# Graph attention on one core: the order of the last two node tiles in layer 2

## The chip, the cores and the metric

The kernel runs on one core of one Trainium2 chip. Its time is the device time of one execution in microseconds (us). Several executions are timed; the median of them is the figure for a kernel, and one further execution is taken with the hardware profiler. Times inside the trace are counted from the first instruction of the program.

## The reference

Two graph-attention (GAT) layers over 3125 nodes and 53125 edges (25000 random pairs in both directions and a self loop for each node, sorted by destination), with a normalisation ahead, a residual product in each layer, and the input added at the end. Cut to what matters:

```python
edge_index = jnp.stack([src, dst])
h = jnp.maximum(_layernorm(x), 0.0)
x = x + _L0_gnn_ref(h, edge_index, ...)

def _L0_gnn_ref(x, ei, ...):
    h0 = x
    h = relu(layer_norm(gat_conv(x, ei, W1, a_src1, a_dst1, b1, heads=4, out_ch=256, concat=True), g1, be1))
    h1 = h + (h0 @ Wr1 + br1)                                   # 3125 x 1024
    h = layer_norm(gat_conv(h1, ei, W2, a_src2, a_dst2, b2, heads=1, out_ch=768, concat=False), g2, be2)
    return h + (h1 @ Wr2 + br2)                                 # 3125 x 768

def gat_conv(x, ei, W, a_src, a_dst, bias, heads, out_ch, concat):
    xl = (x @ W).reshape(n, heads, out_ch)
    # ei as above plus one more self loop for each node
    e = leaky_relu(alpha_src[src] + alpha_dst[dst], 0.2)
    e = exp(e - segment_max(e, dst)[dst])
    alpha = e / (segment_sum(e, dst)[dst] + 1e-16)
    return segment_sum(xl[src] * alpha[:, :, None], dst) + bias
```

## The kernel before, in words

Everything is float32 where it matters here. The nodes are cut into 25 tiles: tiles 0 to 23 have 128 rows, tile 24 has the 53 that are left (`NB`=25, `LAST`=53). Each tile's incoming edges lie in slots of 128 edges: 17 slots for a full tile, 8 for tile 24. Tiles come in chains of three (0,1,2), ..., (21,22,23), (24): within a chain the last slot of a tile is also slot 0 of the next, so it is gathered once.

Layer 1 and the preparation of both layers are untouched by the change. Layer 2 is one block of code at the end, in which the orders of the tensor engine (PE), the vector engine (DVE) and the scalar engine (ACT) are those of the program text (`manual_schedule`). The transfers issued by SP and the indirect gathers issued by POOL are written in the same text and wait by semaphores. The parts of layer 2:

- `residuals`: a generator, one step for each of 8 slices of the product h1 @ Wr2 of a tile. `filled(n)` takes n steps; the loop takes 0, 1, 1, 2 and 4 of them after the five rounds of a tile (`STEPS`), always three tiles ahead (`AHEAD`). Full tiles use `dense` as whole matmuls (L190), tile 24 as 32- and 21-column pieces (L194). It also issues the loads of later h1 and x rows.
- `fetch`: gathers rows of `table2` (768 features and the source score) into a ring of 36 buffers, in the order of the list `slots_due`, on POOL (L210, L214).
- `values`: ACT copies each slot's source score into `slots[b % 2]` (L1365).
- `softmax`: PE transposes the scores (L1383), DVE adds the mask `pen` and takes the maximum (L1387 to L1390, L1392), ACT takes the exponentials (L1391, L1394, L1395). `penalty` prepares the next tile's mask. After a pause PE transposes the weights (L1399); after another DVE and ACT copy them to `w` (L1402, L1403).
- `summed(b, k)`: round k of five: PE sums the gathered rows by their weights into `pa` (L1426). A full tile has 80 of these matmul records in the trace, tile 24 has 36.
- `totals2`: three short DVE operations on the sums of the weights (L1460 to L1462).
- `finish`: a generator: DVE adds the node's own share (L1439) and, after a pause, the bias (L1441), statistics (L514, L516), ACT takes a square root (L520), DVE applies the norm and adds the residual (L1444, L1445), and the result is stored from ACT's queue (L231). For tile 24 the own share was already scaled and given its bias, so that one operation for each half does it (L1449), then L1454 and L1455.
- `own_share`: two POOL operations that scale tile 24's own rows and add the bias (L1467, L1468).
- `load_own`: SP loads a tile's own rows into the one `own` buffer; tile 24's go into a buffer of h1.

The loop over tiles is 0, 1, ..., 24. While tile b is summed, the softmax of b+1 is made at round 2 and its weights are copied after round 4, and `finish(b-1)` runs in pieces at rounds 0, 1 and 2. The step before the last tile is different: in the text of tile 23, tile 24's softmax is begun ahead of round 0 and its weights are copied after round 1. Exponential and square root use different tables of ACT; a table load (`ACT_TABLE_LOAD`) stands where the function changes.

Of the kernel before, what the change touches and what calls it, by code (L numbers as in the profile page):

```python
# [69 lines left out]
def in_order(  # L70
# [1167 lines left out]
    with tc.tile_pool(name="m2", bufs=1, reuse_waits="tile") as mp, \  # L1238
            tc.tile_pool(name="pg2", bufs=1, space=PSUM, reuse_waits="tile") as pp:
        AHEAD = 3  # L1240
        STEPS = [0, 1, 1, 2, 4]
        RING = 36
        f = C2 // 2

        def small(shape, name, dt=F32, bufs=1):
            return mp.tile(shape, dt, name=name, bufs=bufs)
# [59 lines left out]

        def residuals():

            for b in range(NB):
                h1, xr = h1s.pop(b), xrs[b]  # L1310
                r = rows_of(b)
                pm = pp.tile([P, 2, 512], F32, name="pr")
                for k in range(NK2):
                    if k < NK2 // 2:
                        load_h1(b + 2, ks=slice(2 * k, 2 * k + 2))
                    if k in (3, 4):
                        load_xr(b + 1, slice((k - 3) * f, (k - 2) * f))
                    for i in range(2):
                        dense(pm[:, i, :f], h1[:, k, :], wr2[:, k, i * f:(i + 1) * f], r,
                              start=(k == 0), stop=(k == NK2 - 1), at=half_at(b, i).start)  # L1320
                    if k == NK2 - 1 and r == P:
                        nc.vector.tensor_add(pm[:, :, :f], pm[:, :, :f], halves(ball_b))  # L1322
                        nc.vector.tensor_add(halves(xr), pm[:, :, :f], halves(xr))  # L1323
                    elif k == NK2 - 1:
                        nc.vector.tensor_add(xr[:r], xr[:r], ball_b[:r])
                        for i in range(2):
                            cs = slice(i * f, (i + 1) * f)
                            nc.vector.tensor_add(xr[:r, cs], pm[half_at(b, i), i, :f], xr[:r, cs])
                    yield
# [3 lines left out]
        def filled(n):  # L1333
            for _ in range(n):
                next(fill, None)

        gs = {}
        slots_due = [(b, j) for b in range(NB) for k in ROUNDS for j in k
                     if j < tiles_of(b) and not (j == 0 and shared(b))]
        order_of = {s: i for i, s in enumerate(slots_due)}  # L1340
        asked, unused = 0, set(range(len(slots_due)))
# [20 lines left out]
        def values(b, k):  # L1362
            for j in ROUNDS[k]:
                if (b, j) in gs:
                    nc.scalar.activation(slots[b % 2][:, POS[j], :], gs[b, j][:, C2:C2 + 1].to_broadcast([128, 32]), AF.Copy)  # L1365

        def penalty(b):
            if b < NB:
                pen = pens[b] = pens.get(b) or small([128, WIN], "pen")
                nc.scalar.activation(pen, hots.pop(b), AF.Identity, bias=below, scale=BIG)  # L1370
                nc.scalar.activation(pen, pen, AF.Identity, bias=asad2[:, b, 1:2])
                load_hot(b + 2)

        shares = {}

        def softmax(b):

            nonlocal e0, w0
            at, pen = slots[b % 2], pens.pop(b)
            mix = pp.tile([128, 1024], F32, name="mix")  # L1380
            for c in range(WIN // 128):
                o = FROM[c % 4] + c // 4
                nc.tensor.transpose(mix[:, c * 128:(c + 1) * 128], at[:, o:o + 4].rearrange("p q n -> p (q n)"), ident)  # L1383
            top = small([P, 1], "top", bufs=2)
            e, e0 = e0 or small([P, WIN], "e"), None
            sums_ = mix[:, :WIN]
            nc.vector.tensor_tensor_reduce(out=sums_, in0=sums_, in1=pen, scale=1.0, scalar=-BIG,  # L1387
                                           op0=OP.add, op1=OP.max, accum_out=top)
            nc.vector.tensor_scalar(top, top, both[:, b:b + 1], -1.0, op0=OP.max, op1=OP.mult)
            nc.vector.scalar_tensor_tensor(top, top, SLOPE, top, op0=OP.mult, op1=OP.min)  # L1390
            nc.scalar.activation(e, sums_, AF.Copy, scale=SLOPE)  # L1391
            nc.vector.tensor_tensor(e, sums_, e, OP.max)  # L1392
            v = small([P, 4], "v", bufs=3)
            nc.scalar.activation(e, e, AF.Exp, bias=top, accum_out=v[:, 0:1])  # L1394
            nc.scalar.activation(v[:, 1:2], self_s[:, b:b + 1], AF.Exp, bias=top)  # L1395
            penalty(b + 1)
            yield
            for c in range(WIN // 128):
                nc.tensor.transpose(mix[:, c * 128:(c + 1) * 128], e[:, c * 128:(c + 1) * 128], ident)  # L1399
            yield  # L1400
            w, w0 = w0 or small([128, WIN], "w", bufs=2), None
            nc.vector.tensor_copy(w[:, :512], mix[:, :512])  # L1402
            nc.scalar.activation(w[:, 512:], mix[:, 512:WIN], AF.Copy)  # L1403
            shares[b] = w, v
# [26 lines left out]
        def finish(b, pa):  # L1431

            nonlocal z0
            r = rows_of(b)
            own, v = owns.pop(b), shares.pop(b)[1][:r]
            z, z0 = (z0 or small([P, C2], "z", bufs=2))[:r], None
            if b < NB - 1:
                p = pa[:, :, :f]
                nc.vector.scalar_tensor_tensor(p, halves(own), v[:, 2:3], p, op0=OP.mult, op1=OP.add)  # L1439
                yield  # L1440
                nc.vector.scalar_tensor_tensor(p, p, v[:, 3:4], halves(b2_b), op0=OP.mult, op1=OP.add)  # L1441
                yield from norm_steps(mp, p, C2, 1)
                mu, rstd = norm_steps.found
                nc.vector.scalar_tensor_tensor(p, p, mu, halves(g2_b), op0=OP.subtract, op1=OP.mult)  # L1444
                nc.vector.scalar_tensor_tensor(halves(z), p, rstd, halves(xrs.pop(b)), op0=OP.mult, op1=OP.add)  # L1445
            else:
                for i in range(2):
                    cs = slice(i * f, (i + 1) * f)
                    nc.vector.scalar_tensor_tensor(z[:, cs], pa[half_at(b, i), i, :f], v[:, 3:4], own[:r, cs],  # L1449
                                                   op0=OP.mult, op1=OP.add)  # L1450
                yield
                yield from norm_steps(mp, z, C2, 1)
                mu, rstd = norm_steps.found
                nc.vector.scalar_tensor_tensor(z, z, mu, g2_b[:r], op0=OP.subtract, op1=OP.mult)  # L1454
                nc.vector.scalar_tensor_tensor(z, z, rstd, xrs.pop(b)[:r], op0=OP.mult, op1=OP.add)  # L1455
            store_rows(nc.scalar, out, b, z)
# [4 lines left out]
            nc.vector.tensor_scalar(v[:, 3:4], v[:, 0:1], v[:, 2:3], 1e-16, op0=OP.add, op1=OP.add)  # L1461
            nc.vector.reciprocal(v[:, 3:4], v[:, 3:4])  # L1462

        def own_share(b):
            r = rows_of(b)
            own, v = owns[b][:r], shares[b][1][:r]
            nc.gpsimd.tensor_scalar(own, own, v[:, 2:3], v[:, 3:4], op0=OP.mult, op1=OP.mult)  # L1467
            nc.gpsimd.tensor_tensor(own, own, b2_b[:r], OP.add)  # L1468

        with tc.manual_schedule(engines={PE, ACT, DVE}):  # L1470
            penalty(0)
# [12 lines left out]
            values(1, 0)  # L1484
            values(1, 1)
            ending = iter(())
            for b in range(NB):
                pa = pp.tile([P, 2, 512], F32, name="pa", bufs=2)
                opened = set()
                last = b + 1 == NB - 1  # L1490
                for k in range(len(ROUNDS)):
                    if last and k == 0:
                        load_own(b + 1)
                        for i in range(2, len(ROUNDS)):
                            values(b + 1, i)
                        made = softmax(b + 1)
                        next(made)
                    summed(b, k, pa, opened)
                    if k < 2:
                        next(ending, None)  # L1500
                        if 0 < b < NB - 1:
                            load_own(b, slice(k * f, (k + 1) * f))
                    if b + 1 < NB and not last:
                        if k < 3:
                            values(b + 1, k + 2)
                        if k == 2:
                            made = softmax(b + 1)
                            next(made)
                    if k == 2:
                        for _ in ending:  # L1510
                            pass
                    if k == 4:
                        ending = finish(b, pa)
                        next(ending)
                    if b + 1 < NB and k == (1 if last else 4):
                        next(made)
                        next(made, None)
                        totals2(b + 1)
                        if last:
                            own_share(b + 1)  # L1520
                    filled(STEPS[k])
                if b + 2 < NB:
                    values(b + 2, 0)
                    values(b + 2, 1)
            for _ in ending:
                pass

# [471 lines left out]
```

## Time and profile before

| what | value |
|---|---|
| median of 3 timed runs | 1967.19 us |
| the three runs | 1967.47, 1967.19, 1962.85 us |
| the profiled execution | 1958.36 us, span 1956.5 us |
| mean granted PE clock in it | 0.939 |
| busy: PE, DVE, ACT, POOL | 89%, 51%, 23%, 44% of the span |
| DMA | 539.49 MB, mean 276 GB/s |

The span is the time from the first to the last instruction. Layer 2 stands at the end of it, and the two tiles that the change exchanges are worked on in its last 45 us. A row of a timeline has the start and the duration in us, the engine, the line of the kernel, the operation, what it writes and reads, the shape, and how many instructions were merged; in brackets is the idle time of the engine before it and what ended it. PEld are weight loads, and an engine's name with a q is its queue (a transfer that it issues).

### The profile page before, as it was taken

To read this page: it belongs to the slowest core of one execution; us is meant where nothing else is said; L and a number is where in the kernel's file an instruction comes from. 1 tells how busy PE (TensorE), PEld (TensorE's weight loads), DVE (VectorE), ACT (ScalarE), POOL (GpSimd) and SP (SyncE) were. 2 spreads that over 40 slices of the span, in tenths; PEclk is the share of its full clock that TensorE was granted. 3 is DMA by queue.
4 is the path that set the end of the run, shared out by engine and by line. 5 is a ranking of instruction groups with operands and counts; after the bars stand their busy time and mean duration, and the time that the engine had idled before them with its cause. 6 is when DMAs were issued, how large, how long until landed. Compare 5 with 4: busy or idle time off the path is not lost. (4 is left out here: it accounts for less than half of the span.)

```text
span 1956.5 us, 31270 instructions
## 1 busy us (share of the span) xinstructions
PE 1748.2 (89%) x11522; PEld 967.2 (49%) x11522; DVE 1006.5 (51%) x2604; ACT 451.1 (23%) x1312; POOL 854.9 (44%) x892
## 2 busy tenths in 40 slices
PE   8999998999889899899999998938888888888885
PEld 5666665665555454555655544423333334333332
DVE  7673436888654463555655564402334343433436
ACT  2222430001212121211221211212332332333232
POOL 2000112000465544656666666154555565556662
PEclk9999998999899988899999998969888999889897
DMA  7823557331899897999999998596999999899984
GB/s 237 289 96 119 135 162 258 124 120 50 302 369 341 294 349 258 346 345 397 379 381 361 367 382 313 179 345 212 304 301 299 317 321 318 295 315 311 319 284 136
DMA packets 186339, 539.49 MB, mean 276 GB/s; under 512 B 31571, under 2 KB 80083, under 8 KB 186050
## 3 DMA queue, kind: packets, MB, share of 16 engines
q0 software_dynamic: 97328, 379.74, 54.9%
q1 hardware_dynamic: 84456, 147.27, 21.9%
q10 hardware_dynamic: 4394, 10.39, 1.4%
q8 instruction: 94, 1.54, 0.3%
q14 instruction: 67, 0.55, 0.1%
HBM read 483.81 MB, written 65.62 MB: 281 GB/s over the span
## 5 line engine op out<-in xcount | busy, mean ns | idle before, releaser
L210 POOL DMA_INDIRECT g<-table,idx_s x393 | 377.6, 961 | 494.5 <-DVE al L624 175.7
L214 POOL DMA_INDIRECT g<-table,hi_s x407 | 417.8, 1027 | 288.2 <-PE pa L781 134.1
L190 PE MATMUL pr<-wr,h 128*128 128x384 f32 x768 | 288.0, 520 | 28.7 <-DVE xr L1323 22.3
L1426 PE MATMUL pa<-g,w 128*32 128x384 f32 x1956 | 232.6, 524 | 73.4 <-issue 68.1
L781 PE MATMUL pa<-g,w 128*32 128x256 f32 x3912 | 270.5, 392 | 30.5 <-issue 25.2
L190 PE MATMUL p<-w,h1T 128*128 128x384 f32 (+1 forms) x768 | 268.8, 497 | 0.9 <-issue 0.8
L190 PEld LDWEIGHTS pr<-wr,h 128*128 128x128 f32 x768 | 149.6, 205 | 147.0 <-issue 76.8
L781 PEld LDWEIGHTS pa<-g,w 128*32 128x32 f32 x3912 | 124.1, 111 | 168.3 <-issue 81.5
L190 PEld LDWEIGHTS p<-w,h1T 128*128 128x128 f32 x768 | 140.4, 190 | 115.3 <-issue 25.3
L1426 PEld LDWEIGHTS pa<-g,w 128*32 128x32 f32 x1956 | 65.2, 113 | 216.5 <-issue 207.5
L758 DVE TENSOR_TENSOR w<-oh,al 128x128 f32<-128x128 f32 (+1 forms) x416 | 131.7, 317 | 63.9 <-PE pa L781 26.1
L190 PE MATMUL pr<-h0k,wr 128*128 128x256 f32 (+1 forms) x576 | 150.7, 407 | 4.7 <-issue 3.6
L1033 PE MATMUL pm<-h0g,wr 128*128 128x512 f32 x288 | 133.2, 610 | 0.3 <-issue 0.3
L190 PE MATMUL pm<-w,h0g 128*128 128x344 f32 x432 | 131.7, 460 | 0.3 <-ACT h0g L867 0.3
L190 PEld LDWEIGHTS pr<-h0k,wr 128*128 128x128 f32 x576 | 110.5, 199 | 38.4 <-issue 16.5
L190 PE MATMUL pm<-w,h0l 128*128 128x344 f32 x432 | 129.5, 454 | 0.0
L757 DVE TENSOR_SCALAR oh<-iota_f,rel_s 128x32 f32<-128x32 f32 (+1 forms) x416 | 114.5, 275 | 2.9 <-issue 2.6
L1229 DVE COPY asad<-p 128x2 f32<-128x2 f32 (+1 forms) x25 | 4.0, 160 | 201.4 <-ACT row L1227 175.0
L964 POOL DMA_DIRECT2D hot_d<-ohd x25 | 13.4, 536 | 213.0 <-DVE own L531 128.6
L190 PEld LDWEIGHTS pm<-w,h0g 128*128 128x128 f32 x432 | 81.6, 193 | 40.2 <-issue 1.7
L1322 DVE TENSOR_TENSOR pr<-pr,ball_b 128x768 f32<-128x768 f32 x24 | 23.2, 965 | 149.2 <-PE pr L190 72.6
L190 PEld LDWEIGHTS pm<-w,h0l 128*128 128x128 f32 x432 | 80.5, 190 | 39.1 <-issue 0.2
(295 smaller groups left out, 1769.0 us busy)
## 6 DMA issues: line engine op xcount, KB each, us to landing
s<-slo_d SPq DMA_DIRECT2D x25, 544.0 KB
table<-row SPq DMA_DIRECT2D x24, 512.0 KB
own<-table SPq DMA_DIRECT2D x24, 512.0 KB
h1T_d<-h1T SPq DMA_DIRECT2D x24, 512.0 KB
h<-h1T_d SPq DMA_DIRECT2D x88, 128.0 KB
table<-row SPq DMA_DIRECT2D x24, 392.0 KB
ring<-in_x_dram SPq DMA_DIRECT2D x24, 384.0 KB
out_dram<-z ACTq DMA_DIRECT2D x24, 384.0 KB
```

The costliest lines, as they stand in the source:

```text
L190: nc.tensor.matmul(out_, lhsT, rhs, start=start, stop=stop)
L210: nc.gpsimd.indirect_dma_start(out=g, out_offset=None, in_=table[:, :], in_offset=bass.IndirectOffsetOnAxis(ap=idx_s[:, c], axis=0))
L214: nc.gpsimd.indirect_dma_start(out=g, out_offset=None, in_=table[:, :], in_offset=bass.IndirectOffsetOnAxis(ap=idx_k[:, c], axis=0), bound ...
L757: nc.vector.tensor_scalar(oh, iota_f[:, lo:hi], rel_s[:, c:c + 1], None, op0=OP.is_equal)
L758: nc.vector.tensor_tensor(w, oh[:, None, :].to_broadcast([128, heads, hi - lo]), al[:, POS[j], :, b:b + 1].to_broadcast([128, heads, hi - ...
L781: nc.tensor.matmul(pa[p0:p0 + 32, o // f, o % f:o % f + n], w[:, o // cols, :], g[:, o:o + n], start=to not in opened, stop=False, skip_gr ...
L964: nc.gpsimd.dma_start(hot_d[b], ohs[b])
L1033: nc.tensor.matmul(pm, wr1[:, k, m * 128:(m + 1) * 128], groups[gi][:, k, :], start=(k == 0), stop=(k == NK1 - 1))
L1229: nc.vector.tensor_copy(asad2[:r, b, :], pm[half_at(b, i), 384:n])
L1322: nc.vector.tensor_add(pm[:, :, :f], pm[:, :, :f], halves(ball_b))
L1426: nc.tensor.matmul(pa[p0:p0 + 32, i, :f], w_, g[:, i * f:(i + 1) * f], start=(i, q) not in opened, stop=False, skip_group_check=True)
```

## The change

Layer 2 goes through the tiles in a list `ORDER` = 0, ..., 22, 24, 23; `turn(b, n)` is the tile n places after b, and all that was b+1 or b+2 (gathers, residuals, h1 and x loads, masks, scores) follows the list. The special handling of the step ahead of tile 24 is gone: its softmax stands where every tile's does, and its own share is now made by DVE after its totals. For tile 23, which is now the last, all scores, the softmax, the totals and the own share (on POOL) stand in the text behind tile 24's sums and behind the whole of `finish(24)`. A square root whose result nothing reads, `early`, stands in that softmax behind the exponentials. In `finish(23)` a single operation adds the own share, and the result is made and stored in two column halves, the first from ACT's queue, the second from SP's.

```diff
+        ORDER = [*range(NB - 2), NB - 1, NB - 2]
+        at_turn = {b: i for i, b in enumerate(ORDER)}
+        def turn(b, n):
+            i = at_turn[b] + n
+            return ORDER[i] if i < NB else NB
...
-            for b in range(NB):
+            for b in ORDER:
-                        load_h1(b + 2, ks=slice(2 * k, 2 * k + 2))
+                        load_h1(turn(b, 2), ks=slice(2 * k, 2 * k + 2))
-                        load_xr(b + 1, slice((k - 3) * f, (k - 2) * f))
+                        load_xr(turn(b, 1), slice((k - 3) * f, (k - 2) * f))
...
-        slots_due = [(b, j) for b in range(NB) for k in ROUNDS for j in k
+        slots_due = [(b, j) for b in ORDER for k in ROUNDS for j in k
...
             if b < NB - 1:
                 p = pa[:, :, :f]
-                nc.vector.scalar_tensor_tensor(p, halves(own), v[:, 2:3], p, op0=OP.mult, op1=OP.add)
-                yield
-                nc.vector.scalar_tensor_tensor(p, p, v[:, 3:4], halves(b2_b), op0=OP.mult, op1=OP.add)
+                if b == ORDER[-1]:
+                    yield
+                    nc.vector.scalar_tensor_tensor(p, p, v[:, 3:4], halves(own), op0=OP.mult, op1=OP.add)
+                else:
+                    nc.vector.scalar_tensor_tensor(p, halves(own), v[:, 2:3], p, op0=OP.mult, op1=OP.add)
+                    yield
+                    nc.vector.scalar_tensor_tensor(p, p, v[:, 3:4], halves(b2_b), op0=OP.mult, op1=OP.add)
...
+                if b == ORDER[-1]:
+                    for i, q in enumerate((nc.scalar, nc.sync)):
+                        cs = slice(i * f, (i + 1) * f)
+                        nc.vector.scalar_tensor_tensor(z[:, cs], p[:, i], rstd, xr[:, cs], op0=OP.mult, op1=OP.add)
+                        q.dma_start(out[b * P:b * P + r, cs], z[:, cs])
+                    return
...
-            for b in range(NB):
+            for p, b in enumerate(ORDER):
-                last = b + 1 == NB - 1
+                following = turn(b, 1)
+                short = b == NB - 1
                 for k in range(len(ROUNDS)):
-                    if last and k == 0:
-                        load_own(b + 1)
-                        for i in range(2, len(ROUNDS)):
-                            values(b + 1, i)
-                        made = softmax(b + 1)
-                        next(made)
+                    if k == 0 and following == NB - 1:
+                        load_own(following)
                     summed(b, k, pa, opened)
...
-                    if b + 1 < NB and k == (1 if last else 4):
+                    if following < NB and not short and k == 4:
                         next(made)
                         next(made, None)
-                        totals2(b + 1)
-                        if last:
-                            own_share(b + 1)
+                        totals2(following)
+                        if following == NB - 1:
+                            own_share(following, nc.vector)
                     filled(STEPS[k])
+                if short:
+                    load_own(following)
+                    for _ in ending:
+                        pass
+                    for k in range(len(ROUNDS)):
+                        values(following, k)
+                    made = softmax(following)
+                    next(made)
+                    nc.scalar.activation(small([P, 1], "early"), eps, AF.Sqrt)
+                    next(made)
+                    next(made, None)
+                    totals2(following)
+                    own_share(following, nc.gpsimd)
```

More of the change, by code (lines that the diff above doesn't have):

```diff
@@ L1364, in values @@
                 if (b, j) in gs:
-                    nc.scalar.activation(slots[b % 2][:, POS[j], :], gs[b, j][:, C2:C2 + 1].to_broadcast([128, 32]), AF.Copy)
+                    nc.scalar.activation(slots[at_turn[b] % 2][:, POS[j], :], gs[b, j][:, C2:C2 + 1].to_broadcast([128, 32]), AF.Copy)
         def penalty(b):
@@ L1371, in penalty @@
                 nc.scalar.activation(pen, pen, AF.Identity, bias=asad2[:, b, 1:2])
-                load_hot(b + 2)
+                load_hot(turn(b, 2))
         shares = {}
@@ L1378, in softmax @@
             nonlocal e0, w0
-            at, pen = slots[b % 2], pens.pop(b)
+            at, pen = slots[at_turn[b] % 2], pens.pop(b)
             mix = pp.tile([128, 1024], F32, name="mix")
@@ L1395, in softmax @@
             nc.scalar.activation(v[:, 1:2], self_s[:, b:b + 1], AF.Exp, bias=top)
-            penalty(b + 1)
+            penalty(turn(b, 1))
             yield
@@ L1444, in finish @@
                 nc.vector.scalar_tensor_tensor(p, p, mu, halves(g2_b), op0=OP.subtract, op1=OP.mult)
-                nc.vector.scalar_tensor_tensor(halves(z), p, rstd, halves(xrs.pop(b)), op0=OP.mult, op1=OP.add)
+                xr = xrs.pop(b)
+                if b == ORDER[-1]:
[4 more added lines that the diff above has]
+                    return
+                nc.vector.scalar_tensor_tensor(halves(z), p, rstd, halves(xr), op0=OP.mult, op1=OP.add)
             else:
@@ L1462, in totals2, with own_share @@
             nc.vector.reciprocal(v[:, 3:4], v[:, 3:4])
-        def own_share(b):
+        def own_share(b, engine):
             r = rows_of(b)
             own, v = owns[b][:r], shares[b][1][:r]
-            nc.gpsimd.tensor_scalar(own, own, v[:, 2:3], v[:, 3:4], op0=OP.mult, op1=OP.mult)
-            nc.gpsimd.tensor_tensor(own, own, b2_b[:r], OP.add)
+            engine.tensor_scalar(own, own, v[:, 2:3], v[:, 3:4], op0=OP.mult, op1=OP.mult)
+            engine.tensor_tensor(own, own, b2_b[:r], OP.add)
         with tc.manual_schedule(engines={PE, ACT, DVE}):
@@ L1500, in in_order @@
                         next(ending, None)
-                        if 0 < b < NB - 1:
+                        if p and not short and following < NB:
                             load_own(b, slice(k * f, (k + 1) * f))
-                    if b + 1 < NB and not last:
+                    if following < NB and not short:
                         if k < 3:
-                            values(b + 1, k + 2)
+                            values(following, k + 2)
                         if k == 2:
-                            made = softmax(b + 1)
+                            made = softmax(following)
                             next(made)
@@ L1514, in in_order @@
                         next(ending)
-                    if b + 1 < NB and k == (1 if last else 4):
+                    if following < NB and not short and k == 4:
                         next(made)
                         next(made, None)
-                        totals2(b + 1)
-                        if last:
-                            own_share(b + 1)
+                        totals2(following)
+                        if following == NB - 1:
+                            own_share(following, nc.vector)
                     filled(STEPS[k])
-                if b + 2 < NB:
-                    values(b + 2, 0)
-                    values(b + 2, 1)
+                if short:
[4 more added lines that the diff above has]
+                        values(following, k)
+                    made = softmax(following)
+                    next(made)
[4 more added lines that the diff above has]
+                    own_share(following, nc.gpsimd)
+                elif following < NB - 1 and turn(b, 2) < NB:
+                    for k in range(2):
+                        values(turn(b, 2), k)
             for _ in ending:
```

## The prediction

> **What bounds the kernel now.** I read the page's busy shares first, then a table of stretches of the trace cut at the copies of the weights (L1402), one stretch for each tile, then the last 45 us as a timeline. The page and the table, whose columns are the stretch, its length, the busy time of PE, PEld, DVE, ACT and POOL with counts, the granted PE clock, the DMA share and GB/s:
>
> ```profile
> PE 1748.2 (89%) x11522; PEld 967.2 (49%) x11522; DVE 1006.5 (51%) x2604; ACT 451.1 (23%) x1312; POOL 854.9 (44%) x892
> ...
> 1857.90:1887.70 29.80, 25.59 (x137) 11.56 (x137) 10.31 (x20) 8.61 (x27) 16.50 (x18) 0.98 0.86 291
> 1887.70:1912.15 24.45, 19.84 (x150) 6.47 (x152) 10.15 (x21) 8.51 (x27) 14.95 (x16) 0.93 0.86 286
> 1912.15:1927.82 15.67, 10.88 (x105) 5.37 (x95) 10.38 (x21) 8.19 (x27) 7.66 (x8) 0.87 0.65 207
> 1927.82:1950.74 22.92, 13.61 (x126) 5.54 (x126) 18.10 (x37) 5.79 (x19) 2.82 (x2) 0.80 0.21 73
> ```
>
> The 89% of PE is an average. In the stretches of tiles 20 and 21 PE and the transfers fill the time; in the last, from the copy of tile 23's weights to the last result, DVE is busy 18.1 of 22.9 us, the transfers are nearly silent (0.21), and no residual work is left for PE. The change's price is to be read there. The timeline of that stretch:
>
> ```profile
> 1926.90 1.01 DVE L1439 SCALAR_TENSOR_TENSOR pa<-own,v,pa 128x768 f32<-128x768 f32 x1
> ...
> 1927.82 0.68 DVE L1402 COPY w<-mix 128x512 f32<-128x512 f32 x1
> ...
> 1928.85 0.16 DVE L1462 RECIPROCAL v<-v 128x1 f32<-128x1 f32 x1
> ...
> 1929.46 1.33 PE L1383 MATMUL mix<-ident,slots 128*128 128x128 f32 x5 [2.33 <-ACT slots L1365]
> ...
> 1930.72 4.42 PE L1426 MATMUL pa<-g,w 128*32 128x384 f32 x32
> 1931.28 0.83 DVE L1387 CUSTOM_DVE_ANT_0 mix<-mix,pen 128x640 f32<-128x640 f32 x1 [2.26 <-PE mix L1383]
> ...
> 1933.68 1.02 DVE L1441 SCALAR_TENSOR_TENSOR pa<-pa,v,b_b 128x768 f32<-128x768 f32 x1
> ...
> 1934.93 1.28 ACT L520 ACT_TABLE_LOAD   x1
> 1935.07 0.53 PEld L1399 LDWEIGHTS mix<-ident,e 128*128 128x128 f32 x5 [0.62 <-ACT v L1395]
> ...
> 1935.77 7.30 PE L1426 MATMUL pa<-g,w 128*32 128x384 f32 x84
> ...
> 1936.22 0.29 ACT L520 ACTIVATE bn_sd<-bn_mv,eps 128x1 f32<-128x1 f32 x1
> ...
> 1939.91 1.02 DVE L1439 SCALAR_TENSOR_TENSOR pa<-own,v,pa 128x768 f32<-128x768 f32 x1 [0.83 <-PE pa L1426]
> ...
> 1940.97 1.03 DVE L1441 SCALAR_TENSOR_TENSOR pa<-pa,v,b_b 128x768 f32<-128x768 f32 x1
> ...
> 1942.03 1.03 DVE L514 BATCH_NORM_STATS2 bn_st<-pa 128x6 f32<-128x384 f32 x2
> ...
> 1943.81 1.01 DVE L1444 SCALAR_TENSOR_TENSOR pa<-pa,bn_mv,g_b 128x768 f32<-128x768 f32 x1
> 1944.85 1.02 DVE L1445 SCALAR_TENSOR_TENSOR z<-pa,bn_rs,xr 128x768 f32<-128x768 f32 x1
> 1945.78 1.25 DVE L1449 SCALAR_TENSOR_TENSOR z<-pa,v,h 53x384 f32<-53x384 f32 x2
> ...
> 1949.73 1.01 DVE L1455 SCALAR_TENSOR_TENSOR z<-z,bn_rs,xr 53x768 f32<-53x768 f32 x1
> 1950.77 0.95 ACTq L231 DMA_DIRECT2D out_dram<-z  x2
> ```
>
> The reader is to see an overlap. Tile 24's softmax (L1387 at 1931.28, transposes at 1935.07) runs while PE sums tile 23 (1930.72 to 1935.14, and on from 1935.77). Once those weights are there, PE goes through the rest of tile 23 and all of tile 24 in one run of 84 records. After it only DVE work for two tiles is left, ending at 1950.74.
>
> **The change part by part.** I anchor at the same event, the copy of the weights that follows tile 22's sums, at 1927.82. It should keep its place: in tile 22's text tile 24's softmax now stands where tile 23's stood, with 8 score copies for 17, some 0.5 us less at most; I take 0. From there DVE, ACT and PE each follow the new text.
>
> 1. Totals as before: 1928.85 + 0.16 = 1929.01.
>
> 2. The own share of tile 24 moves from POOL to DVE, ahead of `finish(22)`. Its price on DVE comes from a like-sized scaling in layer 1, and from an addition:
>
> ```profile
> L845 DVE TENSOR_SCALAR ring<-ring,bn_mv,bn_rs 53x768 f32<-53x768 f32 x1 | 0.7, 672 | 0.0
> ```
>
> ```profile
> 1913.36 0.95 DVE L1325 TENSOR_TENSOR xr<-xr,ball_b 53x768 f32<-53x768 f32 x1
> ...
> 1937.16 0.98 POOL L1467 TENSOR_SCALAR h<-h,v 53x768 f32<-53x768 f32 x1 [12.25 <-DVE v L1462]
> 1938.22 1.84 POOL L1468 TENSOR_TENSOR h<-h,b_b 53x768 f32<-53x768 f32 x1
> ```
>
> 0.67 + 0.95 = 1.62 us, to 1930.6. Tile 24's 36 records need at most (4.42/32) x 36 = 5.0 us from 1928.5, so they are done by 1933.5, under this DVE work.
>
> 3. DVE then does the rest of `finish(22)` and all of `finish(24)`. That is the sequence seen before from L1441 at 1940.97 to the end of L1455 at 1950.74: 9.77 us, to 1940.4. None of tile 23's softmax is in it, since it stands behind.
>
> 4. ACT has the store of tile 24 next, which waits for L1455: two issues, 0.95 us, to 1941.35. Behind that wait stand all of tile 23's scores. This is the new wait of the change; before, nothing but tile 24's own end was behind such a store.
>
> 5. The scores and the softmax of tile 23, now beside nothing. The rows for it, of the softmax made in tile 22 before:
>
> ```profile
> 1913.04 1.40 ACT L1365 ACTIVATE slots<-g 128x32 f32<-128x32 f32 x11
> ...
> 1922.45 0.83 DVE L1387 CUSTOM_DVE_ANT_0 mix<-mix,pen 128x640 f32<-128x640 f32 x1 [4.58 <-remote]
> ...
> 1924.10 1.28 ACT L1394 ACT_TABLE_LOAD   x1
> ...
> 1925.39 0.83 ACT L1394 ACTIVATE e<-e,top 128x640 f32<-128x640 f32 x1
> ...
> 1926.37 0.76 PE L1399 MATMUL mix<-ident,e 128*128 128x128 f32 x5 [2.22 <-issue]
> ```
>
> 17 score copies at 1.40/11: 2.2 us, to 1943.5. Transposes 1.33 (the row at 1929.46, a half-clock one; see below), and 0.49 from their end to L1387 as there: 1945.3. L1387 to the second transposes 1926.37 - 1922.45 = 3.92, with the table load for Exp in it, since tile 24's square root stands in between: 1949.2. Transposes 1.33 again, the copy 0.05 + 0.68: 1951.3.
>
> 6. Tile 23's 80 records, 80/84 of 7.30 = 6.95 us at the full clock. But PE will have been idle from 1933.5 to 1943.5. The clock in this trace, the same columns as in the first table:
>
> ```profile
> 1927.20:1930.60 3.40, 1.14 (x5) 0.93 (x5) 1.75 (x5) 2.06 (x11) 0.00 (x0) 0.51 0.70 233
> 1930.60:1934.10 3.50, 3.50 (x25) 1.17 (x28) 2.42 (x6) 1.00 (x2) 0.00 (x0) 0.50 0.02 6
> 1934.10:1937.50 3.40, 3.40 (x45) 1.44 (x40) 3.26 (x10) 2.66 (x6) 0.34 (x1) 1.00 0.02 5
> 1937.50:1947.70 10.20, 5.56 (x68) 2.00 (x60) 8.74 (x14) 0.30 (x1) 2.48 (x2) 1.00 0.21 81
> 1947.70:1956.50 8.80, 0.00 (x0) 0.00 (x0) 2.55 (x5) 0.29 (x1) 0.00 (x0) 0.50 0.09 24
> ```
>
> The clock stood at 0.50 while the sums restarted, and came back after one stretch of 3.5 us in which PE was busy throughout. PE's last record ended at 1943.07 and by 1947.7 the clock was halved again. So the sums begin at half rate and lose half of some 3.4 us, 1.7: 8.65 us, to 1959.95. The ends: 6.95 with no loss, (4.42/32) x 80 = 11.05 at half clock throughout. I take the one stretch, as the row at 1930.60 shows.
>
> 7. `finish(23)`: one operation for L1439 and L1441 (1940.97 - 1939.91 = 1.06), from the statistics to L1444 1943.81 - 1942.03 = 1.78, L1444 itself 1.04, two halves at the 1.25 of L1449: 5.13 us, to 1965.1. The own share on POOL, 0.98 + 1.84 = 2.8 us from about 1952.5, is hidden by the sums. If POOL's price grew with 128 rows for 53 it would take 6.8 us and be hidden still.
>
> 8. The early square root saves nothing: the table load at 1934.93 ran ahead of the square root at 1936.22, with no wait for its input, and `finish(23)` would have had the same 10 us to load it in. It costs nothing either, as ACT idles behind the exponentials.
>
> 9. The halves: the last store now has one issue behind the last operation, where two pieces stood (0.95), so 0.4 us less.
>
> The loads and gathers behave the same in kind. Tile 24's own rows are asked for one tile earlier on SP, ahead of tile 22's. The 24 gathers of the last two tiles come in another order, and the last eight are tile 23's, needed only at 1951. Nothing waits on them.
>
> The exchange also reaches tiles 20 and 21: the short tile's residual is made in tile 20's text instead of 21's.
>
> ```profile
> 1873.29 2.85 PE L190 MATMUL pr<-wr,h 128*128 128x384 f32 x8
> ...
> 1900.80 1.47 PE L194 MATMUL pr<-wr,h 128*21 128x384 f32 x16
> ```
>
> A full one is 32 records at 0.356 = 11.4 us, the short one 64 at 0.092 = 5.9, so 5.5 us of PE move from one stretch to the other. The stretches' lengths differ by 29.80 - 24.45 = 5.35, so they follow that work, and the exchange nets to 0; the ends are -5.5 and +5.5, where only one of the two follows it.
>
> **Sum.** 1965.1 - 1950.74 - 0.4 = +13.9 us. The profiled execution took 1958.36, its span 1956.5 and 1.9 around it, so 1972.3 for such an execution. The timed runs lie 4.5 to 9.1 us above the profiled one; carried to their median of 1967.19 that is 1981.1. About 0.3%, 5.9 us, is what a measurement of this kernel can tell from no change.
>
> [...]
>
> **The rivals.**
>
> (a) Not slower: tile 23's scores and maximum get ahead of `finish(24)`, because an engine does not keep the text's order. The point that decides is whether L1387 of tile 23 starts before L1455 of tile 24 ends. Tile 23's sums could then follow tile 24's at 1933.5 and end near 1940.5, and with 5.13 us the last result is there at 1945.6: -5.1, or 1962, no difference that can be told. Against it: L1441 at 1933.68 had its inputs from L1439 at 1927.91 and stood behind tile 24's softmax nonetheless. 6%.
>
> (b) The store does not hold ACT: the scores go ahead behind tile 24's square root, done two DVE operations of 1.0 before the end of L1455, near 1938.3. They end at 1940.5 instead of 1943.5, and L1387 starts 3 us sooner: +10.9, 1978. No row of before has work queued behind such a wait, so it stays open. 13%.
>
> (c) The clock stays halved through tile 23's sums: 11.05 for 8.65, +16.3, 1983.5. [...] 15%. [...]
>
> (d) The residual's exchange does not net to 0: up to 5.5 us either way, 1976 to 1987. 12%.
>
> **How the numbers follow.** The sum as it stands has 54%: 1981, by itself 1976 to 1986 with the spread of the runs. The range reaches down over (b) on the lower timed run (1962.85 + 10.9 = 1973.8), and some 3 us lower for (d) with it, and up over (c) and (d): 1971 to 1988. Left out are (a) and the corners, 2 in 10. Faster by over 0.3% needs (a) together with a gain in (d): 3%. Within 0.3%: the rest of (a), and (b) with (d) downward: 7%. Slower: 90%.
>
> **What would show it.** In the changed kernel's timeline: DVE from L1441 of tile 22 to L1455 of tile 24 in one run of some 10 us with no softmax in it; ACT's 17 score copies only after the store of tile 24; PE idle for some 10 us between tile 24's records and the transposes, and 6 more with two sets of transposes alone; the clock at 0.50 when the 80 records start; the `early` table load off every wait; POOL's two operations over before the records end. The last stretch, copy of weights to last result, should be about 37 us for 22.9. I am wrong if the score copies or L1387 of tile 23 stand under tile 24's sums, or if tiles 20 and 21 together change by several us.

## The result, and the profile after

| | before | after |
|---|---|---|
| median of 16 timed runs each | 1954.86 us (1943.25 to 1967.47) | 1971.70 us (1956.92 to 1980.86) |
| profiled execution, span | 1958.36, 1956.5 us | 1973.55, 1971.3 us |
| mean granted PE clock in it | 0.939 | 0.935 |

The changed kernel is slower: after to before 1.0074, 95% interval 1.0048 to 1.01. On the median of before that is 1954.86 x 1.0074 = 1969.3 us; the two medians themselves lie 16.8 us or 0.86% apart, inside the interval. I had forecast a rise of 0.71% (13.9 on 1967.19) and a time of 1981, range 1971 to 1988. The rise came as forecast. The time did not: 1969.3 lies below the range, and the median of 1971.70 is 9.4 us under the forecast, at the range's lowest edge, because the base on which I set the rise was too high.

The table of stretches of the changed kernel, cut at the copies of the weights (now L1409), columns as before: stretch, length, busy time of PE, PEld, DVE, ACT, POOL, granted clock, DMA share, GB/s. The last row runs to the last result.

```profile
1857.12:1886.43 29.31, 22.49 (x150) 8.88 (x153) 10.26 (x20) 8.62 (x27) 16.73 (x19) 0.85 0.88 303
1886.43:1908.85 22.42, 19.28 (x132) 8.08 (x125) 10.48 (x22) 8.50 (x27) 14.03 (x15) 0.97 0.83 270
1908.85:1928.52 19.67, 14.25 (x106) 6.51 (x104) 10.25 (x20) 7.43 (x18) 8.61 (x9) 0.92 0.67 216
1928.52:1965.73 37.21, 16.26 (x126) 6.18 (x126) 19.05 (x39) 9.42 (x30) 2.80 (x2) 0.68 0.11 38
```

The last stretch has grown from 22.92 to 37.21 us with the same 126 matmul records in it. DVE, busy 18.1 of 22.9 us before, is busy 19.05 of 37.2 now, and the mean clock has fallen from 0.80 to 0.68. The work is nearly the same; it no longer overlaps. The timeline of that stretch shows the order:

```profile
1928.52 0.68 DVE L1409 COPY w<-mix 128x512 f32<-128x512 f32 x1
...
1929.26 4.86 PE L1433 MATMUL pa<-g,w 128*32 128x384 f32 x36 [2.28 <-DVE v L1478]
...
1930.67 0.95 DVE L1486 TENSOR_TENSOR h<-h,b_b 53x768 f32<-53x768 f32 x1
...
1940.22 1.01 DVE L1473 SCALAR_TENSOR_TENSOR z<-z,bn_rs,xr 53x768 f32<-53x768 f32 x1
1941.27 0.95 ACTq L231 DMA_DIRECT2D out_dram<-z  x2
1942.27 2.12 ACT L1372 ACTIVATE slots<-g 128x32 f32<-128x32 f32 x17 [3.18 <-issue]
...
1944.44 1.33 PE L1390 MATMUL mix<-ident,slots 128*128 128x128 f32 x5 [10.32 <-ACT slots L1372]
1945.81 0.83 DVE L1394 CUSTOM_DVE_ANT_0 mix<-mix,pen 128x640 f32<-128x640 f32 x1 [4.57 <-PE mix L1390]
...
1949.72 1.33 PE L1406 MATMUL mix<-ident,e 128*128 128x128 f32 x5 [3.95 <-ACT e L1401]
1949.87 1.28 ACT L1545 ACT_TABLE_LOAD   x1
1951.09 0.69 DVE L1409 COPY w<-mix 128x512 f32<-128x512 f32 x1 [2.79 <-PE mix L1406]
...
1951.84 8.74 PE L1433 MATMUL pa<-g,w 128*32 128x384 f32 x80 [0.78 <-DVE v L1478]
...
1953.47 1.81 POOL L1486 TENSOR_TENSOR own<-own,b_b 128x768 f32<-128x768 f32 x1
...
1964.59 1.14 DVE L1460 SCALAR_TENSOR_TENSOR z<-pa,bn_rs,xr 128x384 f32<-128x384 f32 x2
```

Read the brackets: they are the idle time of the engine ahead of the row. PE idles 10.32 us until tile 23's scores are copied, and those 17 copies (L1372) follow the two store issues of tile 24 at 1941.27. PE then idles 3.95 more for the exponentials. Only then do the 80 records run, 8.74 us where 84 took 7.30 before. The clock of the same stretch:

```profile
1932.20:1939.00 6.80, 1.92 (x20) 0.50 (x12) 5.96 (x12) 0.50 (x2) 0.00 (x0) 1.00 0.15 58
1939.00:1956.10 17.10, 6.92 (x38) 3.24 (x42) 5.30 (x12) 7.07 (x26) 2.80 (x2) 0.50 0.04 11
1956.10:1962.90 6.80, 4.48 (x56) 1.44 (x48) 2.12 (x4) 0.00 (x0) 0.00 (x0) 1.00 0.01 4
```

It is halved from 1939.0, in the long idle time, to 1956.1, some 4 us into the records.

### The profile page after: what moved, and what is told of

Same layout as the page of the kernel before. It is cut to its first block, busy times and chain, and to the rows that moved or that the text cites. A ratio compares the mean times of both kernels' runs of the same rounds, so it can differ in the third digit from the quotient of the medians.

```text
span 1971.3 us, 31276 instructions
## 1 busy us (share of the span) xinstructions
PE 1754.1 (89%) x11522; PEld 964.2 (49%) x11522; DVE 1006.3 (51%) x2606; ACT 453.9 (23%) x1315; POOL 855.3 (43%) x892
## 4 chain that ended last, share of the span: by engine, by line
PE 73%; issue 9%; DVE 8%; another core or an unknown queue 4%; DMA 3%; ACT 2%; POOL 1%; ACTq 0%; DVEq 0%; POOLq 0%
PE pr L190 17%; PE p L190 11%; PE pa L781 11%; PE pm L190 11%; PE pa L1433 9%; PE pm L1033 5%; PE pq L580 3%; PE p L1196 1%; PE mix L1406 1%; DMA g<-table,idx_s 1%; DMA w<-in_L_gnn_W_dram 1%; DMA out_dram<-z 1%; PE mix L1390 1%; PE pt L865 1%
## 5 line engine op out<-in xcount | busy, mean ns | idle before, releaser
L781 PE MATMUL pa<-g,w 128*32 128x256 f32 x3912 | 279.4, 396 | 31.3 <-issue 25.3
L190 PEld LDWEIGHTS pr<-h0k,wr 128*128 128x128 f32 x576 | 108.5, 196 | 37.2 <-issue 16.5
```

The costliest lines, as they stand in the source:

```text
L190: nc.tensor.matmul(out_, lhsT, rhs, start=start, stop=stop)
L781: nc.tensor.matmul(pa[p0:p0 + 32, o // f, o % f:o % f + n], w[:, o // cols, :], g[:, o:o + n], start=to not in opened, stop=False, skip_gr ...
```

## The experiments

Each ratio is to the kernel before, run beside it. "Stretch" is the time from the copy of tile 24's weights to the last result: 22.92 us before (there, the copy that follows tile 22's sums), 37.21 after.

**The scores under the sums.** The order 22, 24, 23 stays; tile 23's softmax goes back under tile 24's sums, `finish(24)` runs in the rounds of tile 23, and the early square root goes away.

```diff
-                if short:
...
+                    if short and k == 0:
+                        load_own(following)
+                        for i in range(len(ROUNDS)):
+                            values(following, i)
+                    if short and k == 1:
+                        made = softmax(following)
+                        next(made)
+                    if short and k == 4:
+                        next(made)
+                        next(made, None)
+                        totals2(following)
+                        own_share(following, nc.gpsimd)
```

> The new order (22, 24, 23) stays, but tile 23's scores and softmax stand under tile 24's sums again: scores behind round 0, the softmax behind round 1, the copy of the weights behind round 4, and finish(24) goes through in the rounds of tile 23. Theory (the +14 us come from the softmax standing behind finish(24) and its store): the last stretch, from the copy of tile 24's weights to the last result, falls from 37.2 to about 23 us, so -14 against the changed kernel and 0 (-2 to +2) against before. Rival 1 (the order itself costs, because a full tile at the end leaves more behind PE's last record): at most half comes back, the stretch stays over 30 us. Rival 2 (the cost lies ahead of that stretch): the stretch shortens but the whole stays more than 8 us above before.

Measured: 1942.86 us, ratio 0.9986 (0.996 to 1.0012). Its timeline:

```profile
1911.05 0.68 DVE L1409 COPY w<-mix 128x512 f32<-128x512 f32 x1
...
1911.94 2.11 ACT L1372 ACTIVATE slots<-g 128x32 f32<-128x32 f32 x17
...
1916.31 0.82 DVE L1394 CUSTOM_DVE_ANT_0 mix<-mix,pen 128x640 f32<-128x640 f32 x1
...
1921.02 0.69 DVE L1409 COPY w<-mix 128x512 f32<-128x512 f32 x1 [0.19 <-PE mix L1406]
...
1932.44 1.14 DVE L1460 SCALAR_TENSOR_TENSOR z<-pa,bn_rs,xr 128x384 f32<-128x384 f32 x2
```

The scores start 0.9 us after the copy for 13.75 in the changed kernel, tile 23's weights are there 10 us after it for 22.6, and the stretch is 22.5 us. All of the loss comes back. So the order 22, 24, 23 by itself costs nothing that can be told; what cost was where tile 23's softmax stands in the text.

**The store that held ACT.** Tile 24's result is stored from SP's queue.

```diff
-            store_rows(nc.scalar, out, b, z)
+            store_rows(nc.sync if b == NB - 1 else nc.scalar, out, b, z)
```

> The changed kernel with one edit: tile 24's result is stored from SP's queue instead of ACT's, so that nothing on ACT waits for L1473. Theory (the store holds ACT): the 17 score copies start right behind tile 24's square root, near 1939 instead of 1942.3 on the changed kernel's time line, and tile 23's maximum follows the end of L1473 by some 1.5 us instead of 4.6: -3.2 us in the last stretch, 37.2 to 34. Rival (DVE's order alone sets it; the store costs nothing): the stretch stays at 37. In the timed runs 3 us are at the edge of what can be told.

Measured: 1952.48 us, ratio 1.0045 (1.0014 to 1.0076), stretch 33.5 us. Its timeline:

```profile
1917.61 0.29 ACT L520 ACTIVATE bn_sd<-bn_mv,eps 53x1 f32<-53x1 f32 x1 [4.60 <-DMA out_dram<-z]
1917.81 2.11 ACT L1372 ACTIVATE slots<-g 128x32 f32<-128x32 f32 x17
```

The 17 copies now follow tile 24's square root at once, where the changed kernel shows `[3.18 <-issue]` ahead of them. Tile 23's weights are copied 19.3 us after tile 24's for 22.6, so 3.3 us of the shorter stretch come from the store: an issue on ACT's queue that waited for DVE held the activations behind it. The other 0.4 us are the 80 records, 8.31 us for 8.74, whose clock came back 3.4 us after their start for 4.3.

**The clock.** Fifteen matmuls whose result nobody reads fill most of PE's idle time, 11 ahead of tile 23's first transposes and 4 between the two sets.

```diff
+                    busy(11)
                     made = softmax(following)
                     next(made)
+                    busy(4)
```

> The changed kernel with 15 added matmuls of ident by rows of wr2, 128x384, whose result nothing reads: 11 ahead of tile 23's first transposes and 4 ahead of its second, where PE is idle for 10.3 and 4.0 us. Theory (PE's idle time halves its clock, and that costs the transposes and the sums): the granted clock reads 1.00 from 1939 to the end of the sums, both sets of transposes take 0.77 instead of 1.33, and the 80 records 7.0 instead of 8.74: -2.9 us in the last stretch. Rival (the clock in the rows is not what bounds these records): the stretch stays at 37.2, or grows if the added matmuls stand in the way.

Measured: 1959.94 us, ratio 1.0058 (1.0031 to 1.0086), stretch 34.0 us, 3.2 less than without them. The 80 records in its timeline:

```profile
1941.71 6.66 PE L1439 MATMUL pa<-g,w 128*32 128x384 f32 x80 [0.78 <-DVE v L1484]
```

6.66 us for 8.74, and each set of transposes 0.76 for 1.33: 2.08 + 2 x 0.57 = 3.2. Of the 14.3 us that the stretch has grown, the held queue takes 3.3 and the half clock 3.2; the 7.8 left are tile 23's softmax standing in line instead of under sums, if the parts add, which no run of both shows. These prices are read from the stretches of single profiles: the timed ratios of these two runs have intervals that overlap the changed kernel's.

**The early load and the halves.** First both are taken out; then, in a further run, the halves alone.

```diff
-                    nc.scalar.activation(small([P, 1], "early"), eps, AF.Sqrt)
...
-                if b == ORDER[-1]:
+                if False:
                     for i, q in enumerate((nc.scalar, nc.sync)):
```

> Of the changed kernel the early square root and the halves at the end are left out; order and own share stay. By my steps 8 and 9 the early table load is worth nothing and the halves 0.4 us, so: copy of tile 24's weights to the last result 37.2 to 37.7 us, about +0.75 to +0.8% on the kernel before. Rival, that the table load for the square root would come to stand between the sums and the last result: +1.3 us more, 38.5.

> The changed kernel with its early square root, its last result stored whole by ACT. Against the run that lacked both, this tells what the early load is worth by itself. Now expected, since the table load stood behind the statistics there: the load off the path again, 37.1 us from the copy of tile 24's weights to the last result (38.8 without the early load), and 4.75 us behind it; +13.5 us, ratio 1.007 (1.004 to 1.010). Rival, that the 38.8 came from the clock alone: 38.8 here too.

Measured without both: 1963.72 us, ratio 1.0107 (1.0073 to 1.0141), stretch 38.8 us. Without the halves alone: 1964.55 us, ratio 1.0104 (1.0067 to 1.0141), stretch 37.2 us. The chain of work that ended last, without both (start, length, engine and line):

```profile
1951.40 0.22 DVE bn_mv L516
1951.62 0.02 issue
1951.64 0.02 ACTq L520
1951.66 0.03 issue
1951.69 0.08 ACT L520
1951.77 1.21 issue
1952.98 0.30 ACT bn_sd L520
```

and in its timeline the table load is `1951.69 1.28 ACT L520 ACT_TABLE_LOAD   x1 [11.48 <-DVE bn_mv L516]`. It waited for the statistics, though ACT had been idle for 11 us: 1.28 us on the path. With the early square root the load stands at 1949.87, under the transposes. The rest of 38.8 - 37.2 is the records, 9.19 us without both and 8.84 without the halves alone. So the early load is worth 1.3 us here, and my step 8 is wrong; the timed ratios of the two runs are too near each other to show it. What tells this load from the one at 1934.93 of the kernel before, which ran ahead, is the `ACTq L520` step: there the square root has a second wait, an instruction of its own on ACT's queue, and the load stands behind that. The trace has three such instructions for L520, the last two of them at the square roots of the last two tiles, where the kernel before (1943.3 and 1948.2 in its trace) had no load to make. The same is seen at tile 24's load where the scores are put back: `1924.62 1.28 ACT L520 ACT_TABLE_LOAD   x1 [2.60 <-DVE bn_mv L516]`. The link is read from the traces; no run took the second wait away.

The halves are not worth their 0.4 us. The span ends 5.57 us after the last result with them (5.42 to 5.50 in other runs that have them), 5.76 and 5.53 in two profiles of the kernel before, and 4.75 and 4.83 where the last result is stored whole from ACT. One issue for 128 full rows comes out 0.6 to 0.8 us ahead of two halves on two queues. The times do not resolve it.

**The residuals.** In the changed kernel tile 22's stretch is 4.0 us longer than before, 19.67 for 15.67, and the last 16 records of a full tile's residual (5.33 us) stood there ahead of its sums. In this run the residuals alone go back to the old order.

```diff
-            for b in ORDER:
+            for b in range(NB):
                 h1, xr = h1s.pop(b), xrs[b]
...
-                        load_h1(turn(b, 2), ks=slice(2 * k, 2 * k + 2))
+                        load_h1(b + 2, ks=slice(2 * k, 2 * k + 2))
...
-                        load_xr(turn(b, 1), slice((k - 3) * f, (k - 2) * f))
+                        load_xr(b + 1, slice((k - 3) * f, (k - 2) * f))
```

> The changed kernel, with the residuals alone made in the old order 22, 23, 24 (their rows are asked for in that order too); the sums stay in the order 22, 24, 23. Theory: the changed kernel's tile 22 waited for the residual made in its text, so its stretch goes back from 19.7 to about 15.7 us, and tile 21's from 22.4 to about 24.5; net -1.5 us (0 to -4), +0.6 to +0.7% on the kernel before. Rival, that the exchange costs nothing net: both stretches move by the same amount, and the time stays at +0.74%.

Measured: 1960.68 us, ratio 1.0073 (1.0041 to 1.0105): the same as the changed kernel's 1.0074. Its stretches of tiles 20, 21 and 22:

```profile
1842.92:1873.46 30.54, 26.16 (x138) 12.24 (x137) 10.27 (x20) 8.61 (x27) 16.70 (x19) 0.95 0.85 296
1873.46:1898.30 24.84, 19.90 (x126) 6.39 (x130) 10.14 (x20) 8.50 (x27) 14.93 (x16) 0.73 0.81 268
1898.30:1915.21 16.91, 11.20 (x122) 4.67 (x114) 10.48 (x21) 7.44 (x18) 7.64 (x8) 0.87 0.67 215
```

Tiles 21 and 22 moved about as I expected, and by itself it proves nothing. The run without early load and halves, whose residuals stand in the new order, shows nearly the same two lengths:

```profile
1875.51:1899.72 24.21, 20.10 (x130) 9.24 (x120) 10.47 (x21) 8.51 (x27) 14.94 (x16) 0.93 0.84 283
1899.72:1916.63 16.91, 10.81 (x98) 4.45 (x96) 10.25 (x20) 7.44 (x18) 7.69 (x8) 0.93 0.64 199
```

That run is the exception, though. Tile 22's stretch is 18.65 to 19.76 us in the other six profiles with the residuals in the new order, and 15.67 to 16.94 in all four with the old one, so the exchange does put some 2.5 us into it. The three stretches together do not tell the orders apart: 69.9 to 72.6 us in the seven, 66.2 to 72.3 in the four, and the 69.9 and 66.2 of two profiles of the kernel before differ by 3.7 on their own. So the exchange moves work into tile 22, and no loss over the three stretches can be told.

> Tile 23's scores and softmax put back under tile 24's sums, with the order 22, 24, 23, the early load and the halves kept, and the residuals in the old order as well. If both reasons hold, about 1.5 us less than with the scores put back alone: ratio to the kernel before 0.998 (0.996 to 1.000). If the exchange nets to 0: 0.9986 as there.

With both the scores and the residuals put back: 1944.09 us, ratio 1.0007 (0.998 to 1.0035). That is no better than the scores alone, and the stretch is 22.5 us in both: no gain from the old order of the residuals shows. The edit left out the early square root as well, which the expectation says it keeps; so did the run with the scores alone.

**The whole store with the scores put back**, the candidate for a kernel better than both:

> As with the scores put back under tile 24's sums (order 22, 24, 23), but the last result is stored whole by ACT and not in halves by ACT and SP. In the run without halves the span ended 4.75 us after the last result, with halves 5.42 to 5.57, and the halves took 0.13 us more of DVE. If that holds: copy of tile 24's weights to the last result 22.4 us, 4.75 behind it, some 0.8 us less than with halves; ratio to the kernel before 0.998 (0.995 to 1.001). Rival, that the 4.75 was an accident of one execution: 5.4 to 5.6 behind the last result.

Measured: 1942.69 us, ratio 0.9999 (0.9972 to 1.0027). The end is 4.85 us behind the last result, as expected, but the stretch is 24.05 us where 22.4 were expected. One row explains it: the same 3.4 us in this run, and in the run with halves.

```profile
1920.70:1924.10 3.40, 2.89 (x20) 0.99 (x24) 3.15 (x9) 0.32 (x2) 2.24 (x2) 0.57 0.32 120
```

```profile
1921.20:1924.60 3.40, 2.83 (x36) 1.20 (x40) 3.20 (x9) 0.28 (x1) 2.19 (x2) 1.00 0.31 120
```

At clock 0.57 PE got through 20 records in 2.9 us, at 1.00 through 36, and all 80 took 8.30 us for 6.66. In this execution the clock took back more than the store gave. No kernel here beats the one before by what the runs can tell.

**The spread of one kernel.** The kernel before again, under a new name:

> The kernel before, unchanged, timed against itself, for the base that the prediction used. Theory (the three runs shown, 1963 to 1967, were the upper end of a spread that comes with the granted clock): the runs spread over 10 us and more, the longer ones at the lower mean clock, about 1.3 us for each 0.001 of clock as in the 16 runs of the changed kernel; ratio 1.000 within 0.3%. Rival (a chip or a day sets the time, and runs on one chip agree): the runs of this call agree within 3 us, with no relation to the clock.

Measured: 1946.48 us, ratio 1.001 (0.9979 to 1.004). Its profile has a span of 1931.7 us, 24.8 less than the profile shown before. Layer 2 in the first profile and in this one, from 1400 us on:

```profile
1400.00:1956.50 556.50, 460.48 (x2596) 203.15 (x2596) 226.04 (x419) 177.82 (x561) 310.35 (x324) 0.90 0.87 293
```

```profile
1400.00:1931.70 531.70, 444.69 (x2572) 194.40 (x2570) 222.91 (x413) 173.61 (x546) 305.14 (x319) 0.92 0.88 302
```

PE is busy 15.8 us longer for 24 more records, some 4 us of work, at a clock of 0.90 for 0.92; the other 9.0 us of the difference are idle time. Over 35 executions of this kernel, from 1928.36 to 1962.82 us, the time falls by 1.43 us for each 0.001 of mean granted clock (correlation -0.87; 1.31 without the two longest); over the 16 of the changed kernel by 1.33 (-0.90). The 12 executions of this run were on one chip and spread over 20 us, so the rival, agreement within 3 us, fell. But the level moved as well: the median of the kernel before was 1946.87 us beside this run and 1943.67 and 1945.02 us beside the two later groups of runs, 8 to 11 us under the 1954.86 of the result. No run shows why.

**Is the clock the cause, or a sign?** The kernel before, with three matmuls of 128x128 behind each of the first four sums of a tile's last round, where PE waits for gathered rows. They go to unused columns of `pa`, but the kernel no longer returns the right result; the time alone is read.

```diff
+                if k == 4 and i == 0 and b < NB - 2:
+                    for _ in range(3):
+                        nc.tensor.matmul(pa[:, 0, 384:512], ident, ident, start=True, stop=True,
+                                         skip_group_check=True)
```

> The kernel before, with three matmuls 128x128 whose results nobody reads behind each of the first four sums of a tile's last round, where PE waits for gathered rows (tiles 0 to 22). One kernel's runs differ by 25 us and follow the mean granted clock with -1.4 us per 0.001. Theory, the clock is the cause: the half-clock stretches that follow this wait in layer 2 become fewer (83 to 117 us of half clock in 1400 to 2000 before), the mean clock rises by 0.01 or more and the time falls by 10 us or more, ratio 0.995 or lower. Rival, the clock only shows how long PE waited for transfers: the clock rises and the time stays (0.998 to 1.003), or grows by what the added matmuls take where nothing is waited for (some 1 us for each tile at most, up to 1.012).

Measured: 2031.03 us, ratio 1.0452 (1.0416 to 1.0488). Both theories miss, the rival's upper end too. From 1400 us on in its trace:

```profile
1400.00:2000.00 600.00, 534.50 (x2992) 256.40 (x2994) 210.66 (x396) 175.25 (x555) 302.01 (x318) 0.94 0.79 265
```

PE was busy 1839.3 us in all, 102 more than in the second profile of before, and the span is 87.8 longer. The transfers were no busier: their share is 0.79 where 0.88 stood. The six timed runs have clocks of 0.948 to 0.954, those of before beside them 0.932 to 0.951, so the clock did rise; but 102 us of added PE time outweigh whatever that brought, and the run does not settle the question it was made for. I had priced the added matmuls at some 1 us for each tile; they took 104.4 us in 23 tiles, 4.5 each. PE's idle time from 1400 us on fell only from 87.0 to 78.8 us, so little of them went into the waits for gathered rows. What the run shows is that PE time added in this part of layer 2 comes out at the end for the most part, 87.8 us for 102. PE time lost to half clock there may count in the same way, which would fit the spread; that the clock is its cause is argued by this, not shown.

## Why the prediction was right and wrong

The steps, as times after the copy of the weights (1927.82 in the sum, 1928.52 in the trace of after):

| step | its end | forecast | measured |
|---|---|---|---|
| 2 | own share of tile 24 on DVE | 2.8 | 3.1 |
| 2 | tile 24's records | 5.7 at most | 5.6 |
| 3 | `finish(24)`, last operation | 12.6 | 12.7 |
| 4 | store issues of tile 24 | 13.5 | 13.7 |
| 5 | tile 23's score copies | 15.7 | 15.9 |
| 5 | copy of tile 23's weights | 23.5 | 23.3 |
| 6 | tile 23's records | 32.1 | 32.1 |
| 7 | last result | 37.3 | 37.2 |

The sum's two terms were +14.3 for the last result and -0.4 for the halves, 13.9. The trace has +14.29, -0.2, and +0.70 by which the copy itself came later: 1971.3 - 1956.5 = 14.8.

**The step that failed is the base.** "The timed runs lie 4.5 to 9.1 us above the profiled one; carried to their median of 1967.19 that is 1981.1." Over 16 executions the median of before is 1954.86, 12.3 us lower and 3.5 under the profiled one; the three runs that I had were the top of a spread of 24 us. The same paragraph has 1972.3, the sum against the profiled execution's own time, and the median measured is 1971.70. I knew four executions, from 1958.36 to 1967.47, and took three of them as the level, though only the profiled one had its granted clock (0.939) beside it. That 1972.3 came so near is luck in part: the profiled execution lay 3.5 us above the median of before, and the medians lie 16.8 apart where the sum had 13.9. My spread of 5 us to each side was too small as well: the changed kernel's runs lie 15 below and 9 above their median.

**The rivals.** (a) fell: L1394 starts at 1945.81, 4.6 us after the last operation of `finish(24)`. (b) fell, and the store on SP shows its price: 3.3 us where I had worked out 3.0. (c) fell: 8.74 us for the 80 records, 8.65 forecast, 11.05 by the rival. Two errors of step 6 cancel in that: at full clock the 80 records take 6.66 us (the run with added matmuls) and not 6.95, and the half clock lasted 4.3 us into them and not 3.4. In five profiles that have such an idle time ahead of them the same records took 8.13 to 9.19 us, with the clock back 3.0 to 5.2 us after their start. The clock's stretches of 6.80, 17.10 and 6.80 us above are close to 2, 5 and 2 times 3.4 us. That the spread of the records comes from where in such a step of 3.4 us they start is my estimate from these lengths; no run tests it. (d) is not borne out: the three stretches have means of 71.5 us in the new order of the residuals and 70.1 in the old, nearer than the 3.7 us by which one kernel's profiles differ, though the single trace of after, at +1.5, could not have said so. The argument for it did not hold, however. I had taken the stretches of tiles 20 and 21 to follow the residual's work; with that work exchanged they are 29.31 us for 29.80 and 22.42 for 24.45, where 5.5 less and 5.5 more were due, and it is tile 22's that grew.

**Where a step held for a wrong reason.** Step 8 gave the early load nothing, since `finish(23)` "would have had the same 10 us to load it in". It would not have used them: 1.28 us were saved. The sum stood because step 7 had no load in it. Step 9's 0.4 us were 0.2 against the first profile of before and nothing against the second (5.57 us for 5.76 and 5.53), with a whole store better than either. The table load took 1.28 us in each row shown here, and without the early load the square root started 0.01 us behind its end (1951.69 + 1.28 = 1952.97, and 1952.98), so 1.28 us are all that the load added there.

## What to carry to other kernels

When a block of work is moved past another in an in-order text, ask what covered it and what stands ahead of it on each queue, a store that waits above all, which took 3.3 us here; the rest of the price here was the cover that was lost, 7.8 us if the parts add, plus the clock that the idle time cost, 3.2 us, and both can be read from rows of the kernel before. Put such a difference on a ratio, and take the base from as many executions as there are with their granted clocks beside them, not from the last few. A stretch that differs between two traces is evidence only when it differs by more than two traces of one kernel do, which here was 3.7 us over three stretches.

## What the runs showed of the hardware that I had not expected

- One kernel's executions spread by 34 us (1928.36 to 1962.82), along the mean granted clock, 1.4 us for each 0.001; whether the clock is the cause stays open.
- A table load ran ahead of a square root that waited in itself (1934.93 in the kernel before), and stood behind a wait that was an instruction of its own: 1.28 us. The link is read from the traces and not tested.
- POOL's two operations on 128 rows (0.99 and 1.81 us) cost what they cost on 53 (0.98 and 1.84).
- A last result of 128 rows stored whole ended 0.6 to 0.8 us earlier than in two halves on two queues, in three profiles against six.
